# Decoder attention: both pairs of heads of the short last block in one pass, and a router that takes rows ahead of their root

## The chip, the cores and the metric

The kernel runs on one core of a Trainium2 chip. A core has TensorE (PE; its weight loads are shown as PEld), VectorE (DVE), ScalarE (ACT), GpSimd (POOL) and SyncE (SP), each with its own queue of instructions, and DMA engines. The metric is device time of one execution in microseconds. Before the change the median of three runs is 2898.42 us (2892.7 to 2900.67).

## The reference

The program is a network of four layers over 2708 rows of 256 numbers. Each layer adds a graph attention over a 2708x2708 adjacency and then a feed-forward block. The change concerns the third layer's feed-forward block, a decoder with grouped attention (four query heads, two key heads of 64 numbers) and a mixture of eight experts, two per row:

```python
def _L2_ffn_ref(x, ln1_w, ln2_w, wq, wk, wv, wo, router_w, w1, w2, w3):
    h = _rmsnorm(x, ln1_w)
    q, k, v = ...                       # 4, 2 and 2 heads of 64, rotary q and k
    scores = jnp.einsum('bhtd,bhsd->bhts', q, k) / jnp.sqrt(jnp.float32(HD))
    scores = jnp.where(causal[None, None], scores, jnp.float32(-1e+30))
    att = jax.nn.softmax(scores, axis=-1)
    y = jnp.einsum('bhts,bhsd->bhtd', att, v).transpose(0, 2, 1, 3).reshape(Bx, Tx, Cx)
    x = x + y @ wo.T
    flat = _rmsnorm(x, ln2_w).reshape(-1, Cx)
    probs = jax.nn.softmax(flat @ router_w.T, axis=-1)
    tp, ti = jax.lax.top_k(probs, TOPK)     # 2 of 8 experts, weights normalised
    ...
    for e in range(NE):
        hh = jax.nn.silu(flat @ w1[e].T) * (flat @ w3[e].T)
        out = out + weights[:, e:e + 1] * (hh @ w2[e].T)
    return x + out.reshape(Bx, Tx, Cx)
```

`_rmsnorm` multiplies a row by the inverse root of its mean square and by a vector of weights. Everything is float32.

## The kernel before

Rows are held in 22 tiles of 128 rows (the last has 20). Attention works on blocks of 512 queries (`chunks(512)`): five blocks of 512 and a last one of 148, which covers tile 20 and the 20 rows of tile 21. The four query heads form two pairs; the two heads of a pair use the two key heads, one in the lower and one in the upper 64 partitions (`halves`).

Three pieces of work make up a block. `project(n)` computes keys, values and the rotated queries of block n; the queries of pair p lie in their own tile `qt{p}`, 128 partitions by 512. `attend(n, p)` goes over the key tiles j that block n may see: two matmuls (L1719) give the scores `sc` of both heads, one exponential on ACT (L1729) makes `e`, the diagonal tiles are masked on DVE (L1732), two matmuls (L1734) add into the outputs `po`, and `e` is added into one of two running sums (L1737): every third tile's on POOL, the others on DVE. At the end matmuls with ones (L1743) give the denominators `pd`, and a reciprocal and a product on DVE (L1745, L1746) write the pair's half of `yt`. `send(n)` takes a finished block on: the output projection `wy`, the residual, the mean squares (ACT, L1764), their inverse roots on DVE (`inverse_root`, a chain of twelve small instructions), the normed rows `h` (L1770), their transposes and the router's matmuls, and then `route.chunk`, which finds the two best experts of each row, counts rows per expert and scatters the rows to their slots in memory by indirect DMAs issued from POOL (L1444).

While `attend` of block n runs, `between` feeds in steps of `project(n+1)` and `send(n-1)`, spread over the key tiles of both pairs, so that their instructions stand between those of attention in each engine's queue. `send` of the last block has nothing to hide behind. After it come the expert matmuls, which read the scattered rows back. When the last `attend` has ended, its memory is released and the third set of expert weights (`w3`) is loaded from SP's queue.

Two score tiles (`sc`) and three `e` tiles circulate; `tp`, `pv`, `wy`, `pr`, `rank` and `pd` share two buffers in PSUM.

Of the kernel before, what the change touches and what calls it, by code (L numbers as in the profile page):

```python
# [8 lines left out]
F32 = mybir.dt.float32  # L9
# [26 lines left out]
def rows(t):  # L36
    return min(P, N - t * P)


def span(t):  # L40
    return slice(t * P, t * P + rows(t))
# [7 lines left out]
def tiles_of(start, length):  # L49
    return range(start // P, (start + length + P - 1) // P)  # L50
# [1559 lines left out]
def attention(net, route, ln2, router, weights):  # L1610
# [3 lines left out]

    nc, tc, a, X = net.nc, net.tc, net.a, net.X
    G, DH = 2, 64
    cols = chunks(512)
    halves = (slice(0, DH), slice(DH, P))  # L1620
    with ExitStack() as ctx:
# [38 lines left out]
        def project(n):  # L1660
            i0, iw = cols[n]
            its = tiles_of(i0, iw)
            rope = pp.tile([P, 2, 512], F32, name="rope")
            nc.scalar.dma_start(rope[:, :, :iw], a["rope"][:, :, i0 : i0 + iw].rearrange("n p i -> p n i"))
            ft = pp.tile([P, 2, 512], F32, name="ft")
            fs = {}
            for t in its:
                fs[t] = pp.tile([P, D], F32, name="f", bufs=4)
                net.normed(fs[t], t, (ln[0], both))
            yield  # L1670
            for k in range(0, len(its), 2):
# [12 lines left out]
            for k, t in enumerate(its):  # L1684
                r = rows(t)
                net.matmul_k(ps[:r, k].rearrange("p g d -> p (g d)"), ft[:, :, k * P : k * P + r], wv)
            for k0, k1, r in whole_and_rest(its):
                nc.scalar.copy(V[:r, its[k0] : its[k1 - 1] + 1], ps[:r, k0:k1])
            queries[n] = [qp.tile([P, 512], F32, name=f"qt{p}") for p in range(2)]
            for dst, w in [(kt[:, i0 : i0 + iw], wk)] + [  # L1690
                (queries[n][p][:, :iw], wq[:, :, p * 2 * P : (p + 1) * 2 * P]) for p in range(2)
            ]:
# [12 lines left out]
        def attend(n, p):  # L1705
            i0, iw = cols[n]
            qt = queries[n][p]
            if p == 0:
                results[n] = rp.tile([P, 2, 512], F32, name="yt")
            po = pso.tile([P, 512], F32, name="po")  # L1710

            sums = [None, None]
            last = tiles_of(i0, iw)[-1]
            for j in range(last + 1):
                r = rows(j)
                o = max(0, j * P - i0)
                ps = psc.tile([P, 2, 512], F32, name="sc", tag="sc")
                for g, b in enumerate(halves):
                    nc.tensor.matmul(ps[:r, g, o:iw], kt[b, span(j)], qt[b, o:iw], start=True, stop=True)  # L1719
                part = j % 3 == 2  # L1720
                new = sums[part] is None
                if new:
                    e = s1.tile([P, 2, 512], F32, name=f"sum{int(part)}", bufs=1 if part else 2)
                    sums[part] = e
                    if o:
                        nc.gpsimd.memset(e[:, :, :o], 0.0)
                else:
                    e = sp.tile([P, 2, 512], F32, name="e")
                nc.scalar.activation(e[:r, :, o:iw], ps[:r, :, o:iw], AF.Exp, scale=DH**-0.5)  # L1729
                if j * P >= i0:  # L1730
                    d = e[:r, :, o : o + r]
                    nc.vector.tensor_tensor(d, d, upper[:r, :r].unsqueeze(1).to_broadcast([r, 2, r]), ALU.mult)  # L1732
                for g, b in enumerate(halves):
                    nc.tensor.matmul(po[b, o:iw], V[:r, j, g, :], e[:r, g, o:iw], start=j == 0, stop=j == last)  # L1734
                if not new:
                    total = sums[part][:r, :, o:iw]
                    (nc.gpsimd if part else nc.vector).tensor_tensor(total, total, e[:r, :, o:iw], ALU.add)  # L1737
                between(p * (last + 1) + j, 2 * (last + 1))
            pd = aux.tile([P, 512], F32, name="pd", tag="aux")
            used = [e for e in sums if e is not None]  # L1740
            for m, e in enumerate(used):
                for g, b in enumerate(halves):
                    nc.tensor.matmul(pd[b, :iw], net.ones[:, :DH], e[:, g, :iw], start=m == 0, stop=m == len(used) - 1)  # L1743
            y = results[n][:, p, :iw]
            nc.vector.reciprocal(y, pd[:, :iw])  # L1745
            nc.vector.tensor_tensor(y, y, po[:, :iw], ALU.mult)  # L1746

        def send(n):
            i0, iw = cols[n]
# [5 lines left out]
            for k, t in enumerate(its):  # L1755
# [57 lines left out]
        for n in range(len(cols)):  # L1813
            steps[:] = 0, 0
            if n + 1 < len(cols):
                waiting.append((last_project if n + 2 == len(cols) else project)(n + 1))
                steps[1] += 7
            if n:
                waiting.append(send(n - 1))
                steps[1] += 14  # L1820
            for p in range(2):
                attend(n, p)
            for rest in waiting:
                for _ in rest:
                    pass
            waiting.clear()
# [332 lines left out]
```

## Time and profile before

| what | before |
|---|---|
| median of three runs | 2898.42 us (2892.7 to 2900.67) |
| profiled execution | 2896.45 us, span 2894.7 us |
| mean granted TensorE clock | 0.946 |
| attention, first to last score matmul | 1664.1 to 2140.1 us |
| last block, from its first po matmul to its last denominator | 2076.4 to 2145.4 us |
| granted clock in that block | 0.77 |
| exponentials of the last block | 42 of 128x296 elements, 0.42 us each, and two small ones |

Times inside the profile are counted from the start of the span. A row of the timeline gives its start, its length, the engine, the line, output and inputs, the shape and how many instructions it merges; in brackets stand the idle time of the engine before it and what ended that. A float32 matmul of the program appears as two matmul records. In the shares by slice and the windows the granted clock is given as a part of full speed.

### The profile page before, as it was taken

The numbers are of one execution on the slowest core, as the hardware profiler recorded it, in microseconds if no ns is written. First come the engines' busy times: TensorE is split into PE (matmuls) and PEld (weight loads), VectorE is DVE, ScalarE is ACT, GpSimd is POOL, SyncE is SP. The second block draws the span as 40 slices with busy tenths as digits, with TensorE's granted clock in tenths as the row PEclk, the third lists the DMA queues.
The fourth block names the chain that finished last, engine by engine and source line by source line (L and its number), as shares of the span: only waits on it lengthen the run. The fifth ranks groups of instructions, "written<-read, shape, count | busy, mean of one in ns | idle before, by whom it ended". The sixth has DMA issues, their size and how long they took to land. (4 is left out here: it accounts for less than half of the span.)

```text
span 2894.7 us, 32765 instructions
## 1 busy us (share of the span) xinstructions
PE 2651.2 (92%) x11893; PEld 1624.4 (56%) x11893; DVE 1441.4 (50%) x3062; ACT 1041.2 (36%) x1658; POOL 369.5 (13%) x462
## 2 busy tenths in 40 slices
PE   6999989799999989878899899998979999969998
PEld 5667746563333334567688433333346677747885
DVE  7753358344777774432644455455543222235455
ACT  3344433224665643211543223233312222215453
POOL 0000012100000001133300123223321111110002
PEclk9999999698999998989999999899969999989999
DMA  8899210000000005354200100002021111041001
GB/s 298 280 292 312 104 65 1 8 1 1 1 1 1 1 19 173 91 166 130 87 1 0 34 22 17 15 0 93 15 101 41 34 30 34 28 137 59 1 1 39
DMA packets 113729, 197.70 MB, mean 68 GB/s; under 512 B 12380, under 2 KB 71636, under 8 KB 110732
## 3 DMA queue, kind: packets, MB, share of 16 engines
q1 hardware_dynamic: 92758, 147.89, 16.1%
q0 software_dynamic: 13120, 38.06, 4.0%
q10 hardware_dynamic: 7690, 9.62, 1.1%
q8 instruction: 99, 1.62, 0.2%
q14 instruction: 62, 0.51, 0.1%
HBM read 135.82 MB, written 59.71 MB: 68 GB/s over the span
## 5 line engine op out<-in xcount | busy, mean ns | idle before, releaser
L675 DVE SCALAR_TENSOR_TENSOR e<-e,mask 128x768 f32<-128x768 f32 (+2 forms) x264 | 411.7, 1574 | 310.9 <-ACT e L674 310.7
L674 ACT ACTIVATE e<-big_p,minus_one,ratio 128x768 f32<-128x768 f32 (+2 forms) x264 | 394.9, 1513 | 363.4 <-PE acc L1236 229.8
L1236 PE MATMUL acc<-V,e 128*128 128x257 f32 (+1 forms) x1936 | 433.5, 383 | 4.5 <-DVE e L675 4.4
L1236 PEld LDWEIGHTS acc<-V,e 128*128 128x128 f32 (+1 forms) x1936 | 352.3, 186 | 85.7 <-issue 32.1
L780 PE MATMUL acc<-e,V 128*64 128x512 f32 (+1 forms) x1056 | 249.7, 550 | 4.1 <-DVE e L675 4.1
L1878 PE MATMUL h<-w,ft 128*128 (+1 forms) x752 | 233.0, 452 | 0.5 <-ACT ft L1860 0.5
L284 PE MATMUL acc<-F,e 128*128 128x257 f32 x968 | 226.3, 384 | 3.3 <-DVE e L281 2.9
L284 PEld LDWEIGHTS acc<-F,e 128*128 128x128 f32 x968 | 173.4, 185 | 67.3 <-DVE e L281 28.7
L780 PEld LDWEIGHTS acc<-e,V 128*64 128x64 f32 x1056 | 95.4, 137 | 180.6 <-issue 159.0
L1719 PE MATMUL sc<-qt,kt 64*128 64x512 f32 (+4 forms) x656 | 187.0, 535 | 4.1 <-ACT e L1729 2.4
L1729 ACT ACTIVATE e<-sc 128x1024 f32<-128x1024 f32 (+4 forms) x140 | 102.8, 760 | 204.5 <-PE sc L1719 188.4
L1878 PEld LDWEIGHTS h<-w,ft 128*128 128x128 f32 x752 | 136.0, 191 | 56.7 <-issue 1.4
L281 DVE TENSOR_TENSOR e<-e,mask 128x512 f32<-128x512 f32 (+2 forms) x132 | 80.4, 625 | 149.4 <-ACT e L275 147.8
L1737 DVE TENSOR_TENSOR sum<-sum,e 128x1024 f32<-128x1024 f32 (+4 forms) x102 | 103.8, 1018 | 99.1 <-ACT e L1729 97.4
L275 ACT ACTIVATE e<-score 128x512 f32<-128x512 f32 (+2 forms) x132 | 69.7, 544 | 179.2 <-PE score L273 153.0
L1734 PE MATMUL po<-e,V 128*64 128x512 f32 (+5 forms) x560 | 119.4, 511 | 14.8 <-ACT e L1729 8.8
L1910 PE MATMUL po<-w,ht 114*128 (+1 forms) x564 | 129.5, 379 | 0.9 <-DVE ht L1903 0.9
L1719 PEld LDWEIGHTS sc<-qt,kt 64*128 64x128 f32 x656 | 71.8, 198 | 94.8 <-issue 80.9
L788 PE MATMUL den<-e,low 128*3 128x512 f32 (+1 forms) x1056 | 123.1, 542 | 0.0
L1910 PEld LDWEIGHTS po<-w,ht 114*128 114x128 f32 x564 | 106.7, 189 | 22.6 <-DVE ht L1903 8.2
L1563 DVE TENSOR_SCALAR second<-f,down 128x1 f32<-128x1 f32 x47 | 10.0, 213 | 213.6 <-DMA f<-hs 213.6
L273 PE MATMUL score<-QK 128*128 128x512 f32 (+2 forms) x264 | 112.1, 554 | 1.2 <-ACT e L275 0.7
(605 smaller groups left out, 3501.0 us busy)
## 6 DMA issues: line engine op xcount, KB each, us to landing
row<-in_adj SPq DMA_DIRECT2D x21, 1354.0 KB
raw<-in_adjT SPq DMA_DIRECT2D x35, 768.0 KB
hs<-zero SPq DMA_DIRECT2D x8, 2838.0 KB
hidden<-hr SPq DMA_DIRECT2D x42, 256.0 KB
wd<-in_f_wd SPq DMA_DIRECT2D x8, 1024.0 KB
kept<-mask SPq DMA_DIRECT2D x21, 338.5 KB
mask<-kept SPq DMA_DIRECT2D x21, 338.5 KB
f<-hs SPq DMA_DIRECT2D x47, 129.0 KB
```

What stands on the lines that cost most here:

```text
L273: nc.tensor.matmul(ps[:r, :iw], QK[:, 0, span(j)], QK[:, 1, i0 : i0 + iw], start=True, stop=True)
L284: nc.tensor.matmul(acc[k][:ri], e[:r, k * P : k * P + ri], F[:r, j, :], start=j == 0, stop=j == NT - 1)
L674: nc.scalar.activation(v, big_p[:, i], AF.Relu, bias=net.minus_one, scale=ratio)
L675: return nc.vector.scalar_tensor_tensor(v, v, 1.0, net.mask[:, j, i], ALU.add, ALU.mult)
L780: nc.tensor.matmul(acc[n][half, :iw], V[:, j, h, :], e[:, k, i0 : i0 + iw], start=j == 0, stop=j == NT - 1)
L788: nc.tensor.matmul(den[g : g + Q, :iw], low[:, j, h, Q - 1 - q : 2 * Q - 1 - q], e[:, k, i0 : i0 + iw], start=False, stop=j == NT - 1 and ...
L1236: nc.tensor.matmul(acc[k][:ri], e[:, k * P : k * P + ri], V[:, j, :], start=j == 0, stop=j == NT - 1)
L1719: nc.tensor.matmul(ps[:r, g, o:iw], kt[b, span(j)], qt[b, o:iw], start=True, stop=True)
L1734: nc.tensor.matmul(po[b, o:iw], V[:r, j, g, :], e[:r, g, o:iw], start=j == 0, stop=j == last)
L1737: (nc.gpsimd if part else nc.vector).tensor_tensor(total, total, e[:r, :, o:iw], ALU.add)
L1878: last = nc.tensor.matmul(halves[s, n][:, q, :HALF], fts[s][:, c, :], weights.w13[n][:, es[s], c, q * HALF : (q + 1) * HALF], start=c == 0 ...
L1910: last = nc.tensor.matmul(po, ht[:KP, k, :], w2[:KP, es[s], k, :], start=k == 0, stop=k == KC - 1)
```

## The change

In the last block both pairs go through `attend` in one pass. Its queries lie in one tile, 128 partitions by two pairs by 148 columns; scores, exponentials, sums and outputs are 296 columns wide instead of 148, for 22 key tiles once instead of twice. `by_pairs` and `by_heads` give the views with the pair as an axis of its own. The steps of `send(4)` that `between` feeds in are spread over 22 key tiles instead of 44. The other blocks keep two passes.

In every `send` the rows that go to the router are now multiplied by ln2's weights alone. Transposes and router matmuls use these, the inverse root is applied to the eight logits of each row when they are copied out of PSUM (one instruction per tile instead of one per pair of whole tiles), and the rows `h` are multiplied by their root afterwards, in place, before `route.chunk`.

```diff
-            queries[n] = [qp.tile([P, 512], F32, name=f"qt{p}") for p in range(2)]
+            if n + 1 < len(cols):
+                queries[n] = [qp.tile([P, 1, 512], F32, name=f"qt{p}") for p in range(2)]
+                pairs = [q[:, 0, :] for q in queries[n]]
+            else:
+                queries[n] = [qp.tile([P, 2, iw], F32, name="qt0")]
+                pairs = [queries[n][0][:, p, :] for p in range(2)]
...
+            m = qt.shape[1]
...
+            steps_of = len(queries[n]) * (last + 1)
+            def by_pairs(t):
+                return t[..., : m * iw].rearrange("p (m i) -> p m i", m=m)
+            def by_heads(t):
+                return t[..., : m * iw].rearrange("p g (m i) -> p g m i", m=m)
...
-                    nc.tensor.matmul(ps[:r, g, o:iw], kt[b, span(j)], qt[b, o:iw], start=True, stop=True)
+                    nc.tensor.matmul(
+                        by_pairs(ps[:r, g])[:, :, o:], kt[b, span(j)], qt[b, :, o:iw], start=True, stop=True
+                    )
...
-                nc.scalar.activation(e[:r, :, o:iw], ps[:r, :, o:iw], AF.Exp, scale=DH**-0.5)
+                ev = by_heads(e[:r])[:, :, :, o:]
+                nc.scalar.activation(ev, by_heads(ps[:r])[:, :, :, o:], AF.Exp, scale=DH**-0.5)
...
-                    nc.tensor.matmul(po[b, o:iw], V[:r, j, g, :], e[:r, g, o:iw], start=j == 0, stop=j == last)
+                    nc.tensor.matmul(
+                        by_pairs(po[b])[:, :, o:], V[:r, j, g, :], by_pairs(e[:r, g])[:, :, o:],
+                        start=j == 0, stop=j == last,
+                    )
...
-                between(p * (last + 1) + j, 2 * (last + 1))
+                between(p * (last + 1) + j, steps_of)
...
-            y = results[n][:, p, :iw]
-            nc.vector.reciprocal(y, pd[:, :iw])
-            nc.vector.tensor_tensor(y, y, po[:, :iw], ALU.mult)
+            y = results[n][:, p : p + m, :iw]
+            nc.vector.reciprocal(y, by_pairs(pd))
+            nc.vector.tensor_tensor(y, y, by_pairs(po), ALU.mult)
...
-            root = inverse_root(net, rp, ss, 1.0 / D, 1e-6, "rr")
-            yield
             for k, t in enumerate(its):
                 r, h = rows(t), hs[t]
-                nc.vector.scalar_tensor_tensor(
-                    h[:r, :D], xs[t][:r], root[:r, k : k + 1], ln2[:r], ALU.mult, ALU.mult
-                )
+                nc.vector.tensor_tensor(h[:r, :D], xs[t][:r], ln2[:r], ALU.mult)
+            yield
+
+            root = inverse_root(net, rp, ss, 1.0 / D, 1e-6, "rr")
             yield
...
-                for k0, k1, r in whole_and_rest(pair):
-                    nc.vector.tensor_copy(route.logits[:r, pair[k0] : pair[k1 - 1] + 1, :], pr[:r, k0:k1, :])
+                for m, t in enumerate(pair):
+                    r = rows(t)
+                    nc.vector.tensor_scalar(
+                        route.logits[:r, t, :], pr[:r, m, :], root[:r, k + m : k + m + 1], None, ALU.mult
+                    )
                 yield
+            for k, t in enumerate(its):
+                r, h = rows(t), hs[t]
+                nc.vector.tensor_scalar(h[:r, :D], h[:r, :D], root[:r, k : k + 1], None, ALU.mult)
...
-            for p in range(2):
+            for p in range(len(queries[n])):
                 attend(n, p)
```

More of the change, by code (lines that the diff above doesn't have):

```diff
@@ L1688, in project @@
                 nc.scalar.copy(V[:r, its[k0] : its[k1 - 1] + 1], ps[:r, k0:k1])
-            queries[n] = [qp.tile([P, 512], F32, name=f"qt{p}") for p in range(2)]
+            if n + 1 < len(cols):
[4 more added lines that the diff above has]
+                pairs = [queries[n][0][:, p, :] for p in range(2)]
             for dst, w in [(kt[:, i0 : i0 + iw], wk)] + [
-                (queries[n][p][:, :iw], wq[:, :, p * 2 * P : (p + 1) * 2 * P]) for p in range(2)
+                (pairs[p], wq[:, :, p * 2 * P : (p + 1) * 2 * P]) for p in range(2)
             ]:
@@ L1707, in attend @@
             qt = queries[n][p]
+            m = qt.shape[1]
             if p == 0:
                 results[n] = rp.tile([P, 2, 512], F32, name="yt")
+            last = tiles_of(i0, iw)[-1]
+            steps_of = len(queries[n]) * (last + 1)
[3 more added lines that the diff above has]
+                return t[..., : m * iw].rearrange("p g (m i) -> p g m i", m=m)
             po = pso.tile([P, 512], F32, name="po")
             sums = [None, None]
-            last = tiles_of(i0, iw)[-1]
             for j in range(last + 1):
@@ L1725, in attend @@
                     if o:
-                        nc.gpsimd.memset(e[:, :, :o], 0.0)
+                        nc.gpsimd.memset(by_heads(e)[:, :, :, :o], 0.0)
                 else:
                     e = sp.tile([P, 2, 512], F32, name="e")
-                nc.scalar.activation(e[:r, :, o:iw], ps[:r, :, o:iw], AF.Exp, scale=DH**-0.5)
+                ev = by_heads(e[:r])[:, :, :, o:]
+                nc.scalar.activation(ev, by_heads(ps[:r])[:, :, :, o:], AF.Exp, scale=DH**-0.5)
                 if j * P >= i0:
-                    d = e[:r, :, o : o + r]
-                    nc.vector.tensor_tensor(d, d, upper[:r, :r].unsqueeze(1).to_broadcast([r, 2, r]), ALU.mult)
+                    for k in range(m):
+                        d = by_heads(e[:r])[:, :, k, o : o + r]
+                        nc.vector.tensor_tensor(d, d, upper[:r, :r].unsqueeze(1).to_broadcast([r, 2, r]), ALU.mult)
@@ L1733, in attend @@
                 for g, b in enumerate(halves):
-                    nc.tensor.matmul(po[b, o:iw], V[:r, j, g, :], e[:r, g, o:iw], start=j == 0, stop=j == last)
+                    nc.tensor.matmul(
+                        by_pairs(po[b])[:, :, o:], V[:r, j, g, :], by_pairs(e[:r, g])[:, :, o:],
+                        start=j == 0, stop=j == last,
+                    )
                 if not new:
-                    total = sums[part][:r, :, o:iw]
-                    (nc.gpsimd if part else nc.vector).tensor_tensor(total, total, e[:r, :, o:iw], ALU.add)
@@ L1738, in attend @@
-                between(p * (last + 1) + j, 2 * (last + 1))
+                    total = by_heads(sums[part][:r])[:, :, :, o:]
+                    (nc.gpsimd if part else nc.vector).tensor_tensor(total, total, ev, ALU.add)
+                between(p * (last + 1) + j, steps_of)
             pd = aux.tile([P, 512], F32, name="pd", tag="aux")
             used = [e for e in sums if e is not None]
-            for m, e in enumerate(used):
+            for k, e in enumerate(used):
                 for g, b in enumerate(halves):
-                    nc.tensor.matmul(pd[b, :iw], net.ones[:, :DH], e[:, g, :iw], start=m == 0, stop=m == len(used) - 1)
@@ L1744, in attend @@
-            y = results[n][:, p, :iw]
-            nc.vector.reciprocal(y, pd[:, :iw])
-            nc.vector.tensor_tensor(y, y, po[:, :iw], ALU.mult)
+                    nc.tensor.matmul(
+                        pd[b, : m * iw], net.ones[:, :DH], e[:, g, : m * iw], start=k == 0, stop=k == len(used) - 1
+                    )
+            y = results[n][:, p : p + m, :iw]
+            nc.vector.reciprocal(y, by_pairs(pd))
+            nc.vector.tensor_tensor(y, y, by_pairs(po), ALU.mult)
         def send(n):
@@ L1790, in send @@
                     net.matmul_k(pr[:r, m, :], ht[:, :, m * P : m * P + r], router)
-                for k0, k1, r in whole_and_rest(pair):
-                    nc.vector.tensor_copy(route.logits[:r, pair[k0] : pair[k1 - 1] + 1, :], pr[:r, k0:k1, :])
+                for m, t in enumerate(pair):
+                    r = rows(t)
+                    nc.vector.tensor_scalar(
+                        route.logits[:r, t, :], pr[:r, m, :], root[:r, k + m : k + m + 1], None, ALU.mult
+                    )
                 yield
+            for k, t in enumerate(its):
+                r, h = rows(t), hs[t]
+                nc.vector.tensor_scalar(h[:r, :D], h[:r, :D], root[:r, k : k + 1], None, ALU.mult)
             yield from route.chunk(rp, aux, its[0], len(its), hs.__getitem__, tag="aux")
```

## The prediction

> **What bounds the kernel now.** I read the page first. TensorE is busy 92% of the span, so what TensorE executes or waits for is the first suspect, and the granted clock stands right beside it.
>
> ```profile
> PE 2651.2 (92%) x11893; PEld 1624.4 (56%) x11893; DVE 1441.4 (50%) x3062; ACT 1041.2 (36%) x1658; POOL 369.5 (13%) x462
> ...
> PEclk9999999698999998989999999899969999989999
> ```
>
> The chain of waits comes next. Its first shown piece in the decoder is the last scatter of rows to expert slots; everything later hangs on it:
>
> ```profile
> 2166.22 0.96 DMA hs<-h,dto
> ```
>
> So a microsecond won before that scatter arrives at the end unless something between takes it back, and the stretch to read is the one before it: the last attention block (2076.4 to 2145.4 us) and its tail (to 2167.2). The busy time by stage shows how it runs:
>
> ```profile
> 2080.00:2100.00 20.00, 18.74 (x140) 11.18 (x138) 12.04 (x33) 7.69 (x24) 6.21 (x8) 1.00 0.00 1
> 2100.00:2120.00 20.00, 18.51 (x152) 12.23 (x152) 10.20 (x31) 6.68 (x17) 3.23 (x4) 0.94 0.00 1
> 2120.00:2140.00 20.00, 19.88 (x91) 11.92 (x90) 6.47 (x26) 4.17 (x10) 7.30 (x8) 0.50 0.08 27
> 2140.00:2160.00 20.00, 9.72 (x43) 4.67 (x42) 8.75 (x39) 1.92 (x7) 5.16 (x6) 0.50 0.75 278
> ```
>
> The columns are length, busy time of PE, PEld, DVE, ACT and POOL, then the granted clock. TensorE fills the block; ACT and POOL are two thirds idle and DVE half. The clock is 1.00 until about 2117 and 0.50 after. The timeline then gives the price of a step. Two steps of 148 columns at full clock, and two of 512 columns in the block before:
>
> ```profile
> 2096.47 0.47 PE L1734 MATMUL po<-e,V 128*64 128x148 f32 x4 [0.25 <-ACT e L1729]
> ...
> 2096.87 0.52 PE L1719 MATMUL sc<-qt,kt 64*128 64x148 f32 x2
> ...
> 2097.72 0.77 PE L1719 MATMUL sc<-qt,kt 64*128 64x148 f32 x6
> ...
> 2098.74 0.47 PE L1734 MATMUL po<-e,V 128*64 128x148 f32 x4 [0.26 <-ACT e L1729]
> ...
> 2053.99 1.08 PE L1734 MATMUL po<-e,V 128*64 128x512 f32 x4 [0.32 <-ACT e L1729]
> ...
> 2059.30 0.65 PE L1734 MATMUL po<-e,V 128*64 128x512 f32 x2 [0.26 <-ACT e L1729]
> ```
>
> 148 columns take 2.27 us for two steps, 512 columns 5.31: three and a half times the columns cost 2.3 times as much, so a 148-column step is largely fixed cost. The end of the block:
>
> ```profile
> 2143.69 0.83 POOL L1737 TENSOR_TENSOR sum<-sum,e 128x296 f32<-128x296 f32 x1
> ...
> 2144.57 0.76 PE L1743 MATMUL pd<-sum,ones 128*64 128x148 f32 x4 [0.53 <-POOL sum L1737]
> 2145.37 1.08 DVE L1745 RECIPROCAL yt<-pd 128x148 f32<-128x148 f32 x1 [4.02 <-PE pd L1743]
> ```
>
> The last denominator waits for a sum on POOL that stands behind the scatters of the previous block.
>
> **Part 1, the merged block on TensorE.** 44 steps of 148 columns become 22 of 296. Between the two measured widths one column costs (5.31-2.27)/364 = 8.35 ns per two steps, so two merged steps take 2.27+148x0.00835 = 3.51 us where four old ones took 4.54: 0.52 us saved per key tile. The order of the changed program has the same grouping of matmuls (one, three, one, three), so I take this value; where four passes stand together the row is 0.45 for the scores and 0.40 for po at 148 columns, which would save only 0.35. 21 full tiles: 10.9 us, or 7.4 by the other rows. The 20-row tile and one set of denominators add about 0.6. Sum -11.5.
>
> ACT, DVE and POOL do the same elements in half as many instructions: the exponential falls from 2x0.42 to about 0.66 us (between 0.42 at 296 and 0.81 at 768 elements), the DVE sum from 2x0.47 to about 0.77, the POOL sum from 2x0.82 to about 1.45. All lie beside TensorE's 1.75 us a tile; I cost them at nothing. Were that cover gone, ACT's 0.66 with its wait of some 0.25 is still in the interpolated period, which already holds 0.25 us of waiting for ACT.
>
> **Part 2, the clock.** From 2117.3 to 2142.1 two steps take 3.54 us (2121.84 to 2125.38) against 2.27. These 24.8 us would be 15.9 at full clock, 8.9 less. Does the merged block keep its clock? The fall came when 148-column steps stood beside the router's 8-column matmuls. Before it, in the block of 512 columns, the same router matmuls ran without a fall. 296 columns stream (by 3.51 against 5.31 us) nearer to the wide case, and the block now ends near the place where the fall came. I take the full 8.9, with 4 to 6 us of it as the loss if the clock falls at the same point of the work.
>
> **Part 3, the last POOL sum.** In the changed order POOL does five scatters of the previous block, then the last sum, then three more; before it did one, a sum, seven, and the last sum. The ranks that these scatters need now come only three full steps before the end. From a rank to its first scatter the trace shows 2.4 us (2129.66 to 2132.09) and 3.4 (2060.31 to 2063.67); five scatters at the 1.27 us between their starts are 6.4, the sum 1.45: the last denominator can run 10.3 to 11.3 us after the rank. TensorE is done after 0.6+3.5+0.8+0.65 = 5.5. It idles about 5.3 us; before, it had 1.8 between the two denominators, partly filled by a wy matmul, which now needs both pairs and cannot fill. Cost +4.0 (bounds +2 and +6). So the block stands at -11.5-8.9+4.0 = -16.4.
>
> **Part 4, the tail.** The router reads rows not yet scaled by their root, so transposes and router run beside the 2.4 us of root on DVE (2150.70 to 2153.13); before, the logits came at 2156.5, 3.4 us after the root. Against that: the reciprocal has 296 columns instead of 148 and is on the path (1.08 at 148, 3.36 at 512: 2.0, +0.9); the product after it +0.15; both halves of wy for both tiles now wait for it, two more calls at some 0.86 us each at half clock (+1.6, or +0.8 at full); ln2's product delays the root by about 0.8 (two at 0.41, the second behind the square on ACT). And two scalings of h at 0.41 stand on DVE between logits and the first maximum, +0.8, in the order of the changed program. Followed instruction by instruction, the first maximum comes 11.4 us after the last denominator, as before (2145.33 to 2156.77). At full clock it would be 2 us earlier. I take -0.3, between +1 and -2. The w3 loads are issued at the end of the last denominator and busy until about 2161.5, before the last scatter at 2167: they move with the block and have some 6 us in hand.
>
> **Part 5, the other sends.** Each send gains four scalings of h (0.41 each) and two small logits (0.2), about 2.0 us of DVE, beside attention, where DVE is half idle. It costs where it delays ranks, then scatters, then the POOL sum at the end of blocks 2 to 4: between 0 (hidden) and 2 us in each of three. I take +1.5. DVE instructions also stretch beside POOL. One of two products of a few hundred ns (L1430) took 2.44 us from 1838.73, while a POOL sum ran from 1838.68 to 1841.02.
>
> The Trainium skill, in "SBUF — State Buffer", section "SBUF: two separate sides", says that certain VectorE operations and a GpSimd operation take an exclusive lock and the loser waits for the whole instruction. The trace agrees at this one row, with the 2.44 us; by that rule each added scaling that meets a POOL sum would wait up to its length, which is the last rival below.
>
> **Sum.** -16.4-0.3+1.5 = -15.2. The profiled execution took 2896.45 us (span 2894.7 and 1.75 around it), 2.0 below the median of the three runs, 2898.42. Forecast 2896.45-15.2 = 2881.
>
> **Rivals.**
> A. The clock falls in the merged block at the same point of the work. Seven tiles are left, 12.3 us at full clock, 19 at half; about 4 to 6 of the 7 show, since the last three tiles lie beside POOL: 2886. For it: at 0.50 the clock stayed from 2117 to 2142 although TensorE was busy. Against: wider steps.
> B. A half-clock stretch of before disappears. After two idle waits (2.0 and 1.2 us at 1840 to 1843, for DVE) the clock was 0.50 for some 28 us, with po at 512 columns taking 1.90 instead of 1.01 us. At ratio 1.88 that is 13 us lost. DVE's order there changes a little; without the stretch: 2868.
> The Trainium skill, "TensorE: Matmul & The Clock Gate", Part 1, says that idling over a window of about 3.4 us halves the clock and a busy window of that length restores it. The fall agrees; the return does not: from 1855 to 1870 PE was busy 5.00 of every 5.00 us and the clock stayed at 0.50.
> C. One more such stretch, at the start of another block where the later POOL sum makes TensorE idle: +13, 2894, which this measurement cannot tell from no change.
> D. Slower: the new scalings of h stall DVE's queue behind POOL sums, with the masks and sums queued behind them, which TensorE waits for. The place is the 16 scalings in the blocks from the second on; each exposed stall costs up to 2.4 us. From seven exposed stalls the gain is gone; with all exposed, +38: 2919. Against it: DVE is half idle and POOL sums cover only a tenth to a fifth of these blocks.
> E. That the router's part does nothing is already in the sum: I give it 0.3.
>
> **How the numbers follow.** Forecast 0.48 (its own range 2874 to 2888 from the bounds of parts 1, 3, 4 and 5), A 0.18, B 0.12, C 0.12, D 0.10. 0.3% is 8.7 us and about what a measurement here can tell from no change: faster means below 2889.7. Faster takes the forecast, A and B less a little of their upper edges, 0.76; same is C and part of D, 0.14; slower is the rest of D, 0.10. The range leaves out D and the tail of B: 2866 to 2894.
>
> **What would show it.** In the changed profile: 22 exponentials of 592 elements; two merged steps 3.3 to 3.7 us apart; clock 1.00 to the end of the block; TensorE idle 4 to 6 us before the last denominator, released by POOL; the block about 53 us instead of 69; the tail to the first maximum 9.5 to 12.5 us. I am wrong if merged steps take over 4 us, if the clock is 0.50 for most of the block, or if blocks 2 to 4 are longer by more than 2 us each.

## The result, and the profile after

The changed kernel takes 2878.12 us (median of 8 runs, 2870.14 to 2886.06) against 2896.28 us for the kernel before (8 runs, 2889.15 to 2900.67): a ratio of 0.9941 with a 95% interval from 0.9929 to 0.9953. On 2896.28 us that is 17.1 us less, between 13.6 and 20.6. The forecast was 15.2 us less, 2881 us.

The profiled execution took 2876.56 us, its span is 2874.8 us, 19.9 us shorter than that of before. Not all of this belongs to the change. The table follows the time through the decoder's attention by four marks that both traces have.

| mark | before, us | after, us | stage length before | after | difference |
|---|---|---|---|---|---|
| first score matmul of the attention | 1664.11 | 1659.18 | 1664.11 | 1659.18 | -4.93 |
| last denominator of block 4 starts: the last block begins | 2075.93 | 2070.93 | 411.82 | 411.75 | -0.07 |
| last reciprocal starts | 2145.37 | 2125.48 | 69.44 | 54.55 | -14.89 |
| first maximum of the last routing (L835) | 2156.77 | 2136.74 | 11.40 | 11.26 | -0.14 |
| end of the span | 2894.7 | 2874.8 | 737.9 | 738.1 | +0.1 |

The program ahead of the attention is the same in both kernels, and its length differs from execution to execution: over the nine profiles of this study the first score matmul came between 1659.2 and 1664.3 us, in kernels that share everything before it. So the first row, 4.9 us, is spread between two executions. The other rows add up to -14.89 - 0.14 - 0.07 = -15.1 us, and nearly all of that lies in the last block. The -0.07 of blocks 0 to 4 is not a sign that nothing happened there: 4.0 us won in blocks 1 and 2 and 4.0 us lost in blocks 3 and 4 cancel in this pair (part 5 below).

The page of the changed kernel, its busy times and its clock by slices:

```profile
PE 2630.7 (92%) x11709; PEld 1604.0 (56%) x11709; DVE 1448.3 (50%) x3078; ACT 1037.4 (36%) x1636; POOL 369.4 (13%) x456
...
PEclk9999999698999998989999999899979999989999
```

TensorE has 184 matmul records fewer and is as busy as before, 92%: it is still the bound. ACT has 22 instructions fewer, those of the merged exponentials. Over the whole span the clock shows the change hardly at all; the stage does. In the chain of waits the last scatter of rows is still the piece on which the rest hangs, 20.1 us earlier:

```profile
2146.15 0.97 DMA hs<-h,dto
```

The busy time by stage (length, then PE, PEld, DVE, ACT, POOL, then the granted clock) over the end of the attention:

```profile
2080.00:2100.00 20.00, 19.18 (x91) 9.14 (x90) 12.59 (x32) 8.13 (x18) 7.92 (x7) 1.00 0.00 1
2100.00:2120.00 20.00, 18.25 (x102) 8.60 (x102) 11.96 (x47) 6.28 (x11) 5.83 (x6) 1.00 0.04 13
2120.00:2140.00 20.00, 8.31 (x30) 4.06 (x27) 9.58 (x38) 1.42 (x5) 7.97 (x9) 0.56 0.75 263
```

From 2080 on the clock is 1.00 to the end of the block's matmuls at 2120.4, all but the last denominator; in before the last 24.8 us of them ran at 0.50. It falls only after that. The timeline of the block, first two merged steps from po to po, then its end:

```profile
2088.36 0.72 PE L1755 MATMUL po<-e,V 128*64 128x296 f32 x4 [0.32 <-ACT e L1749]
...
2091.87 0.72 PE L1755 MATMUL po<-e,V 128*64 128x296 f32 x4 [0.26 <-ACT e L1749]
...
2113.82 0.41 PE L1423 MATMUL rank<-dtaken,dbefore 128*128 128x32 f32 x2
...
2116.50 0.98 POOL L1444 DMA_INDIRECT hs<-h,dto  x1 [1.86 <-DVE h L1442]
...
2119.70 0.72 PE L1767 MATMUL pd<-sum,ones 128*64 128x296 f32 x4
...
2122.68 1.44 POOL L1761 TENSOR_TENSOR sum<-sum,e 128x592 f32<-128x592 f32 x1
...
2124.17 1.25 PE L1767 MATMUL pd<-sum,ones 128*64 128x296 f32 x4 [3.75 <-POOL sum L1761]
...
2125.48 2.01 DVE L1771 RECIPROCAL yt<-pd 128x296 f32<-128x296 f32 x1 [6.33 <-PE pd L1767]
```

From 2088.36 to 2091.87 two merged steps take 3.51 us, which is the interpolated value. From the rank at 2113.82 the line goes over POOL: first scatter 2.68 us later, five scatters until 2122.68, the sum 1.44, and only then the last denominator, for which TensorE stood idle for 3.75 us. In before it waited 0.53 us there.

The next rows are the tail: the product of yt with wo, which can only start after both pairs, then the logits, the two scalings of h, and the first maximum.

```profile
2128.03 3.90 PE L123 MATMUL wy<-wo,yt 128*128 128x256 f32 x8 [2.61 <-DVE yt L1772]
...
2135.94 0.35 DVE L1818 TENSOR_SCALAR dlogits<-pr,rry 128x8 f32<-128x8 f32 x2
2136.22 0.59 DVE L1824 TENSOR_SCALAR h<-h,rry 128x256 f32<-128x256 f32 x2
2136.74 0.15 DVE L835 TENSOR_REDUCE df0m<-dlogits 128x2 f32<-128x16 f32 x1
```

### The profile page after: what moved, and what is told of

Its sections match the earlier page's. It is cut to its first block, busy times and chain, and to the rows that moved or that the text cites. A ratio compares the mean times of both kernels' runs of the same rounds, so it can differ in the third digit from the quotient of the medians.

```text
span 2874.8 us, 32363 instructions
## 1 busy us (share of the span) xinstructions
PE 2630.7 (92%) x11709; PEld 1604.0 (56%) x11709; DVE 1448.3 (50%) x3078; ACT 1037.4 (36%) x1636; POOL 369.4 (13%) x456
## 5 line engine op out<-in xcount | busy, mean ns | idle before, releaser
L1736 PE MATMUL sc<-qt,kt 64*128 64x512 f32 (+5 forms) x568 | 176.6, 574 | 4.1 <-ACT e L1749 2.4
L1749 ACT ACTIVATE e<-sc 128x1024 f32<-128x1024 f32 (+3 forms) x120 | 99.6, 859 | 190.9 <-PE sc L1736 174.4
L1755 PE MATMUL po<-e,V 128*64 128x512 f32 (+3 forms) x480 | 112.2, 549 | 16.8 <-ACT e L1749 8.7
L1736 PEld LDWEIGHTS sc<-qt,kt 64*128 64x128 f32 (+1 forms) x568 | 60.4, 189 | 92.5 <-issue 76.4
```

Of the source, the lines that this page charges most:

```text
L1736: nc.tensor.matmul(by_pairs(ps[:r, g])[:, :, o:], kt[b, span(j)], qt[b, :, o:iw], start=True, stop=True)
L1755: nc.tensor.matmul(by_pairs(po[b])[:, :, o:], V[:r, j, g, :], by_pairs(e[:r, g])[:, :, o:], start=j == 0, stop=j == last,)
```

## The experiments

The theory: the merged steps do less on TensorE, and being wider they keep its clock; the router's part shortens the tail by about what the merging lengthens it; the last POOL sum gives a part back. The rivals: the router's part or its other order of instructions is what keeps the clock, or the gain is a half-clock stretch elsewhere that moved.

### Each half of the change alone

merge_only is the changed kernel with the `send` of before, router_only the kernel before with the changed `send`. The edit that tells them apart (minus is before, plus the change):

```diff
-            root = inverse_root(net, rp, ss, 1.0 / D, 1e-6, "rr")
-            yield
...
-                nc.vector.scalar_tensor_tensor(
-                    h[:r, :D], xs[t][:r], root[:r, k : k + 1], ln2[:r], ALU.mult, ALU.mult
-                )
+                nc.vector.tensor_tensor(h[:r, :D], xs[t][:r], ln2[:r], ALU.mult)
+            yield
...
+            root = inverse_root(net, rp, ss, 1.0 / D, 1e-6, "rr")
```

Both were expected like this:

> The last block takes both pairs in one pass; send keeps the old order (root first, then rows scaled by root and ln2, then transposes and router). My theory (the gain is the merged block: fewer fixed costs per step and a kept clock; the router part only shortens the tail): the block is 54 us as in the changed kernel (68.9 before), two merged steps 3.5 us apart, clock 1.00 to its end; the tail from the last denominator to the first maximum of the routing is about 13.7 us (11.3 in the changed kernel), because the 2.4 us of root stand in line again while the longer reciprocal stays; in all 12 to 13 us faster than the kernel before. Rival 1 (the router part does nothing at all): tail 11.3 us, 15 us faster than before. Rival 2 (the router part's new order of work is what keeps the clock): clock 0.50 for the end of the block, block 58 to 64 us, at most 10 us faster.

> The last block keeps two passes; send has the new order. My theory: the last block stays at 67 to 70 us with the clock at 0.50 from about 2117 on, and the tail from the last denominator to the first maximum falls from 11.4 to about 9.5 us; 2 us faster than before, which the time can hardly tell from no change. Rival 1 (router does nothing): tail 11.4 us, 0. Rival 2 (the router part keeps the clock): clock 1.00 to the end of the block, block about 60 us, 9 to 11 us faster.

And the changed kernel once more, in the same series:

> The changed kernel again, on the chip of the other runs of this call. The two profiles differ by 4.9 us before attention begins, where the programs are the same. If that is spread of executions, the last block is again 54 us and the tail 11.3 us, while the start of attention moves by some microseconds; 15 to 17 us faster than before. If the 4.9 us belong to the change, attention begins again near 1659 us and 20 us are gained.

| kernel | ratio to before (95%) | blocks 0 to 4 | last block | last reciprocal to first maximum |
|---|---|---|---|---|
| before | 1 | 411.8 | 69.44 | 11.40 |
| router_only | 0.9984 (0.9970 to 0.9998) | 412.0 | 70.68 | 9.11 |
| merge_only | 0.9955 (0.9940 to 0.9971) | 415.1 | 53.92 | 13.55 |
| changed_again | 0.9928 (0.9909 to 0.9946) | 411.8 | 54.57 | 11.27 |

Medians: 2890.48, 2882.38 and 2875.26 us, against 2896.82 for before in the same series. Windows of router_only over its last block, as above:

```profile
2100.00:2120.00 20.00, 18.81 (x138) 12.17 (x136) 9.90 (x33) 6.09 (x17) 2.43 (x3) 0.83 0.00 1
2120.00:2140.00 20.00, 19.05 (x94) 11.57 (x92) 6.64 (x27) 3.97 (x11) 9.23 (x10) 0.50 0.12 41
```

and of merge_only:

```profile
2100.00:2120.00 20.00, 18.92 (x102) 9.42 (x104) 10.47 (x36) 6.06 (x10) 4.36 (x3) 1.00 0.00 1
```

The clock goes with the merging: narrow steps fall to 0.50 with the changed router too, wide steps stay at 1.00 with the old one. PE is busy 18.81 and 18.92 of 20 us in the same window, so it is not busy time that differs. The tail goes with the router: 13.55 against 11.27 in the merged kernel, 11.40 against 9.11 in the unmerged one, 2.3 us either way. The reciprocal shows what the merging adds to the tail; of merge_only, then of router_only:

```profile
2129.54 2.01 DVE L1771 RECIPROCAL yt<-pd 128x296 f32<-128x296 f32 x1 [6.34 <-PE pd L1767]
...
2143.09 0.17 DVE L835 TENSOR_REDUCE df0m<-dlogits 128x2 f32<-128x16 f32 x1
```

```profile
2142.91 1.08 DVE L1745 RECIPROCAL yt<-pd 128x148 f32<-128x148 f32 x1 [4.02 <-PE pd L1743]
...
2152.02 0.15 DVE L835 TENSOR_REDUCE df0m<-dlogits 128x2 f32<-128x16 f32 x1
```

By the profiles the merging is worth -15.52 in the block and +2.15 in the tail, -13.4 together, the router +1.24 and -2.29, -1.05. Their sum is -14.4, and the two together gave -15.0 in these two stages: the halves add. merge_only's blocks 0 to 4 took 3.3 us more than before's: 4.0 more in block 4, at whose start the clock was 0.50 between 1960 and 1970 us, and 0.7 less in block 3.

The equal 411.8 of the other rows hide an effect of the router's part. The same stretch in pieces, by the starts of the last denominators of blocks 0, 2 and 4, in the seven profiles whose blocks 1 to 4 have the same sums:

| kernel | send | blocks 1 and 2 | blocks 3 and 4 |
|---|---|---|---|
| before | old | 155.1 | 222.5 |
| merge_only | old | 155.0 | 225.8 |
| two_warm (below) | old | 155.1 | 222.6 |
| changed kernel | new | 151.1 | 226.5 |
| changed_again | new | 151.1 | 226.5 |
| router_only | new | 151.2 | 226.6 |
| last_sum_dve (below) | new | 151.1 | 219.9 |

The new `send` wins 4.0 us in blocks 1 and 2 in every profile, 3.1 of them in block 1. At its end, the two rank matmuls of before, then those of the changed kernel:

```profile
1758.34 0.41 PE L1423 MATMUL rank<-dtaken,dbefore 128*128 128x32 f32 x2 [0.61 <-DVE dtaken L1414]
...
1760.67 0.64 PE L1424 MATMUL rank<-dso_far,ones 128*128 128x32 f32 x2
```

```profile
1752.60 0.41 PE L1423 MATMUL rank<-dtaken,dbefore 128*128 128x32 f32 x2
...
1752.84 0.39 PE L1424 MATMUL rank<-dso_far,ones 128*128 128x32 f32 x2
```

In before they stand 2.33 us apart and the clock is 0.63 between 1758 and 1762; in the changed kernel they stand 0.24 us apart and the clock is 1.00 between 1752 and 1756. merge_only and two_warm, with the old `send`, repeat the one picture, the kernels with the new one the other; how much is the wait for DVE and how much the clock was not separated. With these 4.0 us the router's part is worth about -5 us, and its time says -4.6 (-0.6 to -8.7). Blocks 3 and 4 differ by up to 6.7 us, and by 6.5 between two kernels with the same code there (changed kernel and last_sum_dve).

The second execution of the changed kernel repeats the block and the tail within 0.02 us, while its attention starts at 1660.80 us instead of 1659.18: these two stages repeat far better than the whole does. Its time is 20.9 us below before (15.6 to 26.4), where 15 to 17 were expected.

### The last POOL sum moved to VectorE

```diff
-                part = j % 3 == 2
+                part = j % 3 == 2 and (m == 1 or j < last - 2)
```

The last third sum of the merged block, which stands behind the five scatters, is added on DVE into the other sum.

> The changed kernel, but the last sum of the merged block that stood on POOL behind five scatters (key tile 20) is added on DVE. My theory (TensorE's 3.75 us idle before the last denominator are the price of that place in POOL's queue): the idle falls below 1 us, the block to about 50 us; 4 us faster than the changed kernel, 19 us faster than before. With TensorE idle for less, the clock may also stay higher in the tail, 1 to 2 us more. Rival (something else is late next: DVE with two more instructions between masks and sums, or the scatters, which now finish as late as before): idle falls by less than 2 us, or the tail is longer by what the block gains; 0 to 2 us against the changed kernel.

The timeline of last_sum_dve at the block's end:

```profile
2117.35 0.78 DVE L1761 TENSOR_TENSOR sum<-sum,e 128x592 f32<-128x592 f32 x1
...
2118.61 1.22 PE L1767 MATMUL pd<-sum,ones 128*64 128x296 f32 x8
2119.88 2.01 DVE L1771 RECIPROCAL yt<-pd 128x296 f32<-128x296 f32 x1 [1.39 <-PE pd L1767]
```

All denominators now run in one go with no wait for POOL, and the block takes 50.31 us instead of 54.55: 4.24 us were lost to that sum, as expected. The tail is 0.9 us shorter as well (10.37): the clock is 1.00 from 2119 to 2128, while wy runs, where the changed kernel had 0.50 from 2125 to 2135. The time, 2871.47 us and a ratio of 0.9924 (0.9908 to 0.9940), overlaps that of the change itself (0.9928 in the same series); some 5 us cannot be told apart by the times here, only by the trace.

### All late POOL sums moved

```diff
-                part = j % 3 == 2
+                part = j % 3 == 2 and j < last - 2
```

In every block the last third sum goes to DVE.

> The changed kernel, but in every block the sums of the last three key tiles are added on DVE, none on POOL, so that no last denominator stands behind scatters. In the changed kernel TensorE is idle 25.2 us before denominators for a POOL sum, in nine places, 3.75 us of them in the last block. My theory: these idle times are on the path and they also pull the clock down at the starts of blocks 3 and 4. Idle before denominators falls to 4 to 8 us; attention from its first score matmul to the start of the last block takes 385 to 400 us instead of 411.8 and the last block 50 us; 18 to 28 us faster than the changed kernel, 35 to 45 us faster than before. Rival (DVE is late instead: its queue holds the masks, the sums and the routing, and it is half busy): the denominators wait for DVE sums as long as they did for POOL; 4 to 8 us faster than the changed kernel.

What TensorE waited for ahead of the denominators (L1767; us, places), in the changed kernel:

```profile
  POOL sum L1761: 25.2, 9
```

and in all_sums_dve:

```profile
  issue: 7.2, 17
  DVE sum L1761: 1.8, 3
```

The waits for a POOL sum are gone; all waits there together are 10.1 us, a little over the 4 to 8 expected. From the first score matmul to the last reciprocal of block 4 the attention takes 394.1 us instead of 413.5, from there to the last reciprocal 46.6 instead of 52.8. The time is 2855.66 us (5 runs, 2852.08 to 2859.07; before in this series 2899.97), a ratio of 0.9851 (0.9832 to 0.9869): 43 us faster than before, and by the ratios 22 to 26 us faster than the change (0.9928 and 0.9941). This version beats both kernels. Of the 19.4 us in blocks 0 to 4, 7.6 may not be the edit's: they lie in block 3, in a half-clock stretch that last_sum_dve was without too, though nothing was changed there (see the rivals). Another 1.8 come from block 0, whose only POOL sum is the moved one, so that its second sum and eight denominator records fall away. The clock is 1.00 from 1845 to 2100 here, where the changed kernel had 0.84 between 1845 and 1900 and short falls later. What the waits and what the clock gave of the rest was not separated by a run.

### The tail's two scalings and the halves of the reciprocal

On top of all_sums_dve, the scalings of h go to ACT and the reciprocal and product of the last block are done pair by pair, so that wy may start after the first.

```diff
-            y = results[n][:, p : p + m, :iw]
-            nc.vector.reciprocal(y, by_pairs(pd))
-            nc.vector.tensor_tensor(y, y, by_pairs(po), ALU.mult)
+            for k in range(m):
+                y = results[n][:, p + k, :iw]
+                nc.vector.reciprocal(y, by_pairs(pd)[:, k])
+                nc.vector.tensor_tensor(y, y, by_pairs(po)[:, k], ALU.mult)
...
-                nc.vector.tensor_scalar(h[:r, :D], h[:r, :D], root[:r, k : k + 1], None, ALU.mult)
+                nc.scalar.activation(h[:r, :D], h[:r, :D], AF.Copy, scale=root[:r, k : k + 1])
```

> As the run with all last sums on DVE, and in addition the rows of every send are scaled by their root on ACT instead of DVE, and the last block's reciprocals and products are made for one pair after the other. My theory: the tail from the start of the last reciprocal to the first maximum falls by 0.6 us (two scalings off DVE) and by up to 1 us (wy starts with the first pair while the second is divided): 8.8 to 9.8 us where the run with the last sum on DVE had 10.4; 1 to 2 us against the run with all sums on DVE, which the time can hardly tell. Rival (ACT's scalings stand before exponentials and cost TensorE waits in the blocks): attention longer by 1 to 4 us, no gain.

The tail falls from 11.62 to 10.54 us: the difference of 1.1 is as expected, the length is not (8.8 to 9.8). all_sums_dve's tail was already longer than last_sum_dve's 10.37, at a clock of 0.53 between 2103 and 2113. The time, 2855.72 us and 0.9851 (0.9834 to 0.9868), does not show it.

### Does the narrow block keep its clock with full-array matmuls in it?

The kernel before, with one unused matmul of 128 rows by 256 columns after every second step of its last pass from tile 6 on, eight in all (work that the result does not need):

```diff
+                if n + 1 == len(cols) and p == 1 and j >= 6 and j % 2 == 0:
+                    warm = aux.tile([P, 2, 2 * P], F32, name="tp", tag="aux")
+                    nc.tensor.matmul(warm[:, 0, :], net.ident, kt[:, : 2 * P], start=True, stop=True)
```

> The kernel before, with one extra full-array matmul (identity by 256 columns of the keys, result not used) at every second key tile from 6 on in the second pass of the last block: eight extra matmuls of about 0.5 us at full clock. It asks whether the half clock at the end of the block hangs on how full TensorE's array is, and what it costs. My theory (narrow 64-row matmuls let the clock fall and stay down): the clock stays at 1.00 to the end of the block and two steps without an extra matmul take 2.3 us; the block falls from 69.4 to about 64 us though it holds 4 us more work; 4 to 6 us faster than before. Rival (the fall comes from the waits in that stretch, or the clock stays down whatever runs): clock 0.50 from about 2117 on, block about 76 us, 7 us slower than before.

The windows of two_warm over the stretch that ran at 0.50 in before:

```profile
2100.00:2120.00 20.00, 18.33 (x156) 12.04 (x154) 10.56 (x35) 5.59 (x16) 3.27 (x4) 1.00 0.01 1
2120.00:2140.00 20.00, 12.38 (x93) 6.40 (x89) 5.47 (x21) 3.30 (x9) 10.58 (x11) 0.83 0.20 63
```

and its timeline, two steps with one such matmul, and the end of the block:

```profile
2115.45 0.47 PE L1734 MATMUL po<-e,V 128*64 128x148 f32 x4 [0.27 <-ACT e L1729]
2115.86 0.70 PE L1737 MATMUL tp<-kt,ident 128*128 128x256 f32 x2
...
2117.98 0.47 PE L1734 MATMUL po<-e,V 128*64 128x148 f32 x4 [0.32 <-ACT e L1729]
...
2130.36 0.47 PE L1746 MATMUL pd<-sum,ones 128*64 128x148 f32 x4
...
2136.93 0.76 PE L1746 MATMUL pd<-sum,ones 128*64 128x148 f32 x4 [5.47 <-POOL sum L1740]
```

With the extra work the clock stays at 1.00 until TensorE is done, and two steps take 2.53 us (2115.45 to 2117.98) where before took 3.54 at half clock. TensorE reaches its first late denominator 59.0 us after the block's start instead of 66.2. But now it waits 5.47 us for the POOL sum instead of 0.53. The block takes 66.4 us, 3.0 less than before and 2.4 more than the 64 expected, and the time is 2897.08 us, a ratio of 0.9995 (0.9983 to 1.0006): no change that the time can show, where 4 to 6 us were expected. (In this profile the part after the first maximum took 742.0 us, in the other eight 736.6 to 738.5; why is not known.) So the gain of the clock and the wait for POOL are not two separate terms: what TensorE wins is first spent on POOL's queue, whose scatters hang on a rank that does not come earlier by as much.

## Why the prediction was right

**Part 1, merged steps: right in its price, too large at the head of the block.** Two steps take 3.51 us, as interpolated. But 0.52 us a tile holds only after the first six. TensorE's timeline of the block's head in before, the start of the first step's po, and that of the twelfth:

```profile
2075.93 1.44 PE L1743 MATMUL pd<-sum,ones 128*64 128x512 f32 x4 [2.35 <-POOL sum L1737]
2077.15 0.71 PE L1734 MATMUL po<-sum,V 128*64 128x148 f32 x4
...
2094.19 0.47 PE L1734 MATMUL po<-e,V 128*64 128x148 f32 x4
```

and the same in the changed kernel, whose sixth step is the one at 2088.36 shown above:

```profile
2070.93 1.69 PE L1767 MATMUL pd<-sum,ones 128*64 128x512 f32 x4 [2.35 <-POOL sum L1761]
2072.40 1.21 PE L1755 MATMUL po<-sum,V 128*64 128x296 f32 x4
2073.54 1.22 PE L123 MATMUL wy<-wo,yt 128*128 128x256 f32 x2
2074.69 1.27 PE L1736 MATMUL sc<-qt,kt 64*128 64x296 f32 x8
```

Twelve narrow steps from the block's start took 18.26 us, the six wide ones 17.43: 0.8 saved where the working has 6 x 0.52 = 3.1. Two things stand in these rows. The head runs at half clock after the idle wait of 2.35 us, and there a wide step loses more (po 1.21 against 0.72 us later) than a narrow one (0.71 against 0.47). And the wy matmuls of the previous block fall in it: in before 5.6 us of them lengthened 11 steps by 4.55 us (17.04 - 11 x 1.135), the rest lying in waits for ACT; in the changed kernel 5.3 us of them, with the half clock, lengthened 5 steps by 7.2 (15.96 - 5 x 1.755). That these two cost the 2.3 us is argued from the rows; how it divides between them was not run.

**Part 2, the clock: right.** The full 8.9 us was taken, and the clock held; merge_only and router_only show that the merging holds it. The reason given, that wider steps stream nearer to the wide case, is supported by two_warm, where fuller work in the same narrow steps did the same; it is not shown to be the width itself.

**Part 3, the last POOL sum: right in mechanism and cost, the wait itself too long.** TensorE stood 3.75 us, a quarter of a microsecond under the 4 to 6 announced. The queue took 10.35 us from the rank to the denominator, the lower end of 10.3 to 11.3; and TensorE was done 6.6 us after the rank, not 5.5, since the po of tile 20, the last whole one, waited 0.67 us for the masks on DVE, which the working left out. The cost taken, 4.0, against the 4.24 us that last_sum_dve wins back.

**The block, -16.4 forecast, -14.89 measured.** The head gave -0.8 instead of -3.1. From there to the start of the last denominator the sum had -13.3 (the other 16 tiles and the denominators 8.4, the clock 8.9, POOL against it 4.0); measured are 35.81 us instead of 50.38, -14.6, 1.3 better, about what the wait for POOL was shorter (3.75 instead of 5.3). The last denominator itself, twice as wide, took 0.5 more. The step that failed is the uniform 0.52 us for each tile, used in a stretch where the steps are not alone on TensorE.

**Part 4, the tail: right.** 11.26 us against 11.40, -0.14 where -0.3 was taken. merge_only and router_only show the two sides of 2.3 us each that cancel. The two scalings of h cost less than 0.41 each: 0.59 for both.

**Part 5, the other sends: wrong, and hidden by luck.** +1.5 was taken for the added work on DVE, and blocks 0 to 4 took 411.75 us instead of 411.82. That is not the lower bound, hidden, coming true. The new order won 4.0 us in blocks 1 and 2, in all four kernels of the table that have it; the working priced only the added instructions and not what becomes of the ranks when the order changes. And this pair lost 4.0 us in blocks 3 and 4, of which 3.0 in block 4. Its start in before, then in the changed kernel:

```profile
1965.40 1.08 PE L1743 MATMUL pd<-sum,ones 128*64 128x512 f32 x4 [3.37 <-POOL sum L1737]
...
1966.41 1.98 PE L1719 MATMUL sc<-qt,kt 64*128 64x512 f32 x6
```

```profile
1957.39 1.08 PE L1767 MATMUL pd<-sum,ones 128*64 128x512 f32 x4 [3.37 <-POOL sum L1761]
...
1958.40 3.59 PE L1736 MATMUL sc<-qt,kt 64*128 64x512 f32 x6
```

The wait is the same, 3.37 us, but the scores after it take 3.59 instead of 1.98: the clock is 0.62 between 1957 and 1964 here and 1.00 between 1965 and 1972 in before. Over the kernels with unchanged sums blocks 3 and 4 took 219.9 to 226.6 us, so this loss is not shown to be the change's. The scalings themselves take 0.35 us each in the blocks, where 0.41 was taken.

**The rivals.** A, the clock falling in the merged block, did not occur. B, the half-clock stretch of 1840 to 1870 vanishing, did not occur in the profiles of the change: the stretch is there, shifted. (It is two stretches, of 10 and 17 us, with a clock of 0.93 between 1851 and 1855 in before; and of the two waits that were read there only the first, 2.0 us, is one of the matmuls for DVE, the second stands at the weight loads.) The second stretch also goes without the change. last_sum_dve differs from the changed kernel in the last block alone, and its blocks 0 to 4 took 405.3 us instead of 411.8, with block 3 shorter by 7.6 and block 4 longer by 1.1. In the changed kernel, the wait ahead of the stretch and the clock after it (timeline, then windows):

```profile
1832.93 1.55 PE L1755 MATMUL po<-e,V 128*64 128x384 f32 x4 [2.12 <-DVE e L1753]
```

```profile
1850.00:1860.00 10.00, 10.00 (x20) 2.97 (x20) 2.46 (x4) 2.89 (x4) 0.00 (x0) 0.50 0.00 0
```

and in last_sum_dve:

```profile
1838.09 1.55 PE L1755 MATMUL po<-e,V 128*64 128x384 f32 x4 [2.12 <-DVE e L1753]
```

```profile
1850.00:1860.00 10.00, 9.69 (x34) 2.77 (x30) 6.21 (x6) 3.44 (x4) 0.00 (x0) 1.00 0.01 2
```

The same wait of 2.12 us stands in both; 17 to 27 us after it the clock is 0.50 in the one, and in the other 1.00 from 12 us on. What decides it was not found; it comes and goes in unchanged code. A short stretch that the forecast did not name, of 3.4 us at the end of block 1, did vanish with the new `send`. C, one more stretch, occurred at the start of block 4 (part 5), at a cost of 3.0 us instead of 13 and after a POOL sum that was no later than before; the 4.0 us of blocks 1 and 2 hide it. D, scalings that stall DVE's queue beside POOL sums, was not put to the test: none of the 22 scalings in the changed kernel overlaps a sum or product on POOL. E, the router's part, was in the sum with 0.3 us; it does 2.3 in the tail, of which 2.15 pay for the merged tail, and 4.0 in blocks 1 and 2.

The terms that were off cancel: +1.5 in the block, -1.4 in parts 4 and 5, and within part 5 the 4.0 us won and lost. So -15.2 forecast against -15.1 in the profiles is closer than the working deserves. What followed the edit in every profile, the last block, the tail and blocks 1 and 2, is -14.9 - 0.1 - 4.0 = -19.0 us, which lies in the intervals of both times, -17.1 (-13.6 to -20.6) and -20.9 (-15.6 to -26.4). The bounds of the parts, added up, give 2876 to 2892 us, not the 2874 to 2888 that the forecast calls its own range; both hold the measured 2878.

## What to carry to other kernels

Price a step from rows at the same width and clock, but ask of each stretch of it what else stands on the engine there: at the head of a block, where other matmuls fill the waits, half as many steps save little. When TensorE is made faster, look for the sum, scatter or rank on a slow engine's queue that its last result needs; here that queue took back 4 us of this change and 4 of the 7 us that TensorE won in two_warm, and moving the sums to an engine with room was worth more than the change itself. And compare stages between common marks, not spans: kernels with the same code there differed by up to 5 us before the attention began and by 6.5 us in its first five blocks. A stage whose length did not change can still hold a gain and a loss; cut it further, and over several kernels, before calling a term zero.

## What was not expected of the hardware

The granted clock does not follow TensorE's busy time alone. With 148-column steps of 64 rows PE was busy 19.05 of 20 us at a clock of 0.50 (router_only, 2120 to 2140); with the same steps and one 128-row, 256-column matmul in two of them it was busy 18.33 of 20 at 1.00 (two_warm, 2100 to 2120), and with 296-column steps 18.25 of 20 at 1.00 (the change). Nor did the fall need idle time: in before PE was busy 3.50 of 3.50 us from 2113.5 to 2117.0, and the clock was 0.58 in the 3 us after; in router_only it was busy 3.50 of 3.50 from 2109.5 to 2113.0, and the clock was 0.53 in the 3.5 us after. In both, the router's 8-column matmuls stand in that busy stretch. The runs fit a clock that hangs on how much of the array streams rather than on whether an instruction is running, but this was not shown: the quantity that decides was not measured, and the 512-column steps of the changed kernel, too, stayed at 0.50 between 1850 and 1860.

The Trainium skill, "TensorE: Matmul & The Clock Gate", Part 1, lets the gate follow how busy the PE has recently been, with a window of some 3.4 us of work to restore it. Here the trace disagrees: 10.00 of 10.00 us busy between 1850 and 1860 us in the changed kernel, shown above, left the clock at 0.50. Nor does the fall agree, as the prediction has it: a clock of 0.65 between 1840 and 1843.4 in before puts the fall at 1841.0, some 1.1 us into the wait of 2.0.
